# K and V by seven products of blocks for pairs of head groups, in a cross-attention and feed-forward block on one core

## The chip, the cores and the metric

One core of one Trainium2 chip runs the whole program; nothing is sharded. The metric is the device time of one run in microseconds, the median of the runs shown. Five engines work side by side, each through its own list of instructions in order: PE (TensorE, matmuls), DVE (VectorE), ACT (ScalarE), POOL (GpSimd) and SP (SyncE, which here only issues transfers). They wait for each other by semaphores.

## The reference

Four sequences (`B`) of 512 rows of width 512, 16 heads of 32, and a feed-forward width of 2048, all in f32:

```
q = (layer_norm(x, ln1) @ q_w + q_b)          # heads of 32
k = (encoder @ k_w + k_b)
v = (encoder @ v_w + v_b)
attn = softmax(where(mask, q k^T / sqrt(32), min))
hidden = (attn v) @ cproj_w + cproj_b + x
y = gelu(layer_norm(hidden, ln2) @ fc_w + fc_b)
out = hidden + y @ proj_w + proj_b
```

## The kernel before

The 16 heads of a sequence form four groups of four heads, 128 columns of Q, K and V each; `w` counts groups over all four sequences, 0 to 15, so groups 0 to 3 are sequence 0. The context `eT` and the normalized rows `xT` lie transposed in `ext`, the weights of a group in `ptt` (`kqv_w`, two slots each for K, Q and V), K and Q of four groups in `pbt` (`k_q`), V of five groups in `mix` (`v_of`).

For each group K, Q and V are made with four matmuls of 512 columns for K and Q (L475, L487) and sixteen of 128 columns for V (L497). ACT copies K and Q with their bias (L477, L489) and V (L502) out of the bank, and POOL adds V's bias (L330). For each of four blocks of 128 query rows, PE then makes the scores of four heads, one bank each of `sc` (L510); DVE adds the mask and takes the maximum (L518), ACT the exponential and its sum (L521); DVE transposes in blocks of 32 (L529, L536, L539) into one of two buffers, half a group each. POOL copies the blocks that stay on their partitions (L546, the stay step), SP's transfers exchange the others, and PE multiplies with V (L568), which DVE scales (L574).

After a sequence's attention come the output projection (L443), the second normalization with its transposes (L369), and the feed-forward layer. The latter already uses seven products of blocks where plain blocks would take eight: `a_sums` and `b_sums` form sums of blocks of both operands, four each (the weights' on POOL, L330 and L333, the rows' on DVE); `fc` makes seven products of 128 x 256 x 256, five in one bank as a chain whose value is read out after the first, third, fourth and fifth, and two in another; `joins` copies the chain at each of those points on ACT (L646, L651) and adds the other bank on DVE. A product of the chain may only be added once the copy ahead of it has read the bank. A chunk of 256 hidden columns is joined in a `stage` buffer, goes through gelu (L667) there, and leaves for DRAM (L669); three such buffers go round. Four `acc` banks serve everything but the scores. The last layer (`project`) uses such products on two levels.

The order in which every engine's instructions are written is one long table, `ORDER`: a token names a step and each time that it appears the step's generator runs on by one `yield`. Since each engine works in order, the table fixes what stands ahead of what.

Of the kernel before, what the change touches and what calls it, by code (L numbers as in the profile page):

```python
# [12 lines left out]
F32 = mybir.dt.float32  # L13
# [47 lines left out]
s1:0 k:0 s1:0 s1:0 s1:0 r1:0 n1:0 n1:0 n1:0 n1:0 wq:1 wv:1 k:0 v:0 k:1 k:1 qb t1:0:1 t1:0:1 t1:0:0 t1:0:3 t1:0:0  # L61
  t1:0:2 m:0 t1:0:2 t1:0:3 q:0 q:0
u:0:0 x:0:0 x:0:0 x:0:0 x:0:0 q:1 r:0:0
u:0:1 r:0:0 lx:1 lf:0:0 lf:0:0 wq:2 wv:2 v:1 wk:3 wk:2 lx:1 lx:1 lc wv:3 lf:0:2 v:0 x:0:1 x:0:1 x:0:1 x:0:1 r:0:1
  r:0:1 q:1
u:0:2 r:0:1 r:0:1 q:2 x:0:2 x:0:2 x:0:2 x:0:2
u:0:3 r:0:2 x:0:3 x:0:3 v:1 x:0:3 v:3 x:0:3
u:1:0 k:3 v:2 e:0:0 e:0:0 e:0:0 lh:0 lh:0 wq:3 r:0:2 r:0:3 r:0:3 lx:1 wv:5 m:0 d:0:0 v:1 d:0:0 x:1:0 s1:1 r:0:3 r:0:3
  e:0:1 e:0:1 e:0:1 v:3 s1:1 x:1:0 x:1:0 x:1:0 r:1:0 r:1:0
u:1:1 k:2 x:1:1 x:1:1 x:1:1 v:2 x:1:1 k:2 r:1:1 s1:1  # L70
u:1:2 r:1:1 q:2 s1:1 x:1:2 x:1:2 x:1:2 x:1:2 k:3 d:0:1 d:0:1 v:0 fs:0:0 r:1:2 r:1:1 q:3
u:1:3 r1:1 a:0:0 ts:1 r:1:1 x:1:3 ts:1 le:1 wk:4 wq:4 wk:5 lt:1 lt:1 le:1 le:1 le:1 a:0:1 a:0:0 x:1:3 e:1:0 ts:1 k:4
# [12 lines left out]
u:4:0 k:7 d:3:0 d:3:0 a:2:1 r:3:2 r:3:3 r:3:3 m:1 r:3:3 r:3:3 x:4:0 x:4:0 x:4:0 x:4:0
u:4:1 r:4:0 v:7 x:4:1 x:4:1 x:4:1 v:6 e:3:1 e:3:1 wv:9 e:3:1 lf:0:2 x:4:1 v:6
u:4:2 r:4:0 r:4:1 a:3:0 x:4:2 x:4:2 k:7 r:4:1 a:3:0 x:4:2 r:4:1 r:4:1 x:4:2 c:0:1 d:3:1 v:4 d:3:1
u:4:3 r:4:2 c:0:0 a:3:1 x:4:3 x:4:3 q:7 x:4:3 c:0:1 r:4:3 x:4:3 c:0:0
u:5:0 r:4:2 r:4:3 x:5:0 x:5:0 a:3:1 x:5:0 x:5:0 c:0:2
u:5:1 c:0:3 s2:0 r:4:3 wk:8 lh:0 d:4:0 cb:0 c:0:2 s2:0 s2:0 r:4:3 le:2 lx:2 le:2 lf:0:1 wq:6 s1:2 wk:9 lh:0 e:4:0  # L90
  e:4:0 e:4:0 le:2 le:2 c:0:0 v:7 fs:0:0 fs:0:0 cb:0 d:4:0 fs:0:1 x:5:1 c:0:3 fs:0:0 m:1 v:6 c:0:1 d:4:1 e:4:1 q:6
  wv:8 e:4:1 e:4:1 d:4:1 x:5:1 r:5:0 x:5:1 x:5:1 a:4:0
u:5:2 v:9 k:8 s2:0 r:5:0 x:5:2 r2:0 r:5:1 n2:0 r:5:1 n2:0 r:5:1 r:5:1 q:6 x:5:2 x:5:2 k:8 x:5:2 c:0:2 c:0:3 n2:0
u:5:3 a:4:0 n2:0 x:5:3 t2:0:1 t2:0:1 r:5:2 t2:0:0 t2:0:0 x:5:3 r:5:2 x:5:3 k:9 a:4:1 x:5:3 r:5:3 v:9 k:9 y:0
u:6:0 x:6:0 d:5:0 fs:0:1 fs:0:1 d:5:0 t2:0:3 t2:0:2 x:6:0 t2:0:2 x:6:0 x:6:0 a:4:1 v:8 f:0:0 t2:0:3 j:0:0 r:5:3 r:5:3
  y:0
u:6:1 y:0 f:0:0 f:0:1 f:0:0 e:5:0 lx:2 wk:10 lx:2 s1:2 lt:2 lt:2 e:5:0 e:5:0 lf:0:3 r:5:3 e:5:1 lx:2 x:6:1 y:0 v:8
  r:6:0 x:6:1 f:0:1 j:0:0 f:0:0 x:6:1 j:0:0 j:0:1 x:6:1 r:6:0
u:6:2 f:0:1 j:0:1 j:0:0 f:0:0 f:0:1 j:0:0 x:6:2 s1:2 r:6:1 r:6:1 j:0:1 f:0:2 fs:0:1 fs:0:2 d:5:1 fs:0:2 s1:2 r1:2
  x:6:2 j:0:1 f:0:1 j:0:1 x:6:2 j:0:0 x:6:2 r:6:1 ts:2 a:5:0 a:5:0 j:0:1 r:6:1  # L100
u:6:3 g:0:0 g:0:0 ts:2 g:0:1 x:6:3 x:6:3 j:0:2 lf:0:4 e:5:1 wk:11 lt:2 lf:0:4 e:5:1 wv:10 wq:8 e:6:0 fs:0:2 d:5:1 k:10
  ts:2 fs:0:2 fs:0:3 lb:2 e:6:0 lb:2 d:6:0 fs:0:3 d:6:0 f:0:2 f:0:2 r:6:2 x:6:3 x:6:3 r:6:2 r:6:3 j:0:2 k:10 r:6:3
  r:6:3
u:7:0 f:0:2 j:0:2 x:7:0 x:7:0 x:7:0 x:7:0 a:5:1
u:7:1 fs:0:4 e:6:0 v:10 wv:11 lf:0:5 a:5:1 r:6:3 e:6:1 lh:1 lf:0:5 x:7:1 v:10 x:7:1 r:7:0 lt:2 fs:0:4 fs:0:3 na:2
  g:0:0 na:2 na:2 fs:0:4 d:6:1 cb:1 a:6:0 x:7:1 x:7:1 wa:2 r:7:0 r:7:1 j:0:2 a:6:0 r:7:1
u:7:2 f:0:4 j:0:4 x:7:2 f:0:4 f:0:4 x:7:2 j:0:4 f:0:2 f:0:4 j:0:2 x:7:2 wa:2 j:0:4 fs:0:4 f:0:3 x:7:2 j:0:4 f:0:4
  r:7:1 e:6:1
u:7:3 na:2 g:0:1 j:0:4 wa:2 wa:2 g:0:4 r:7:1 j:0:4 q:8 q:8 g:0:4 d:6:1 d:7:0 d:7:0 e:6:1 lf:0:6 lf:0:6 fs:0:6 g:0:4
  f:0:3 lh:1 lh:1 e:7:0 e:7:0 e:7:0 x:7:3 x:7:3 r:7:2 x:7:3 x:7:3 a:6:1  # L110
u:8:0 a:6:1 j:0:2 r:7:3 r:7:2 m:2 x:8:0 r:7:3 j:0:3 x:8:0 v:11 x:8:0 x:8:0 r:7:3 a:7:0 wq:9 wq:10 lx:3
u:8:1 f:0:3 r:7:3 a:7:0 j:0:3 v:11 x:8:1 s1:3 e:7:1 fs:0:3 lf:0:7 e:7:1 e:7:1 r:8:0 x:8:1 d:7:1 cb:1 g:0:1 x:8:1 x:8:1
  r:8:1 c:1:1 c:1:1 f:0:3 g:0:2 q:10
u:8:2 q:9 r:8:0 r:8:1 r:8:1 x:8:2 j:0:3 r:8:1 q:9 x:8:2 q:10 x:8:2 x:8:2
u:8:3 d:7:1 v:8 j:0:3 f:0:3 f:0:5 k:11 x:8:3 x:8:3 r:8:2 r:8:2 j:0:3 e:8:0 wq:11 lf:1:0 e:8:0 le:3 le:3 lh:1 e:8:0
  a:7:1 j:0:3 r:8:3 x:8:3 x:8:3 g:0:3 r:8:3 r:8:3
u:9:0 d:8:0 fs:0:5 fs:0:5 cb:1 d:8:0 fs:0:5 g:0:2 v:10 g:0:2 c:1:1 x:9:0 x:9:0 x:9:0 a:7:1 x:9:0 j:0:5 k:11 c:1:0
  r:8:3 c:1:0
u:9:1 x:9:1 x:9:1 r:9:0 f:0:5 f:0:5 j:0:5 fs:0:5 d:8:1 fs:0:6 fs:0:6 d:8:1 cb:1 s2:1 wk:13 e:8:1 wv:12 lx:3 e:8:1 lx:3
  lf:0:7 lf:1:0 wq:12 e:8:1 wv:13 lf:1:1 f:0:7 f:0:5 c:1:3 j:0:5 r:9:1 x:9:1 x:9:1 j:0:5 f:0:5  # L120
# [119 lines left out]
def xattn_block(ctx: ExitStack, tc: tile.TileContext, x, x_t, encT, mask, q_w, k_w, v_w, c_w, w_fc, p_w, vecs, rows, out):  # L240
# [679 lines left out]
```

## Time and profile before

| what | us |
|---|---|
| median of three runs | 760.3 |
| lowest and highest | 758.3 and 760.86 |
| the profiled execution, its own time | 759.81 |
| its span, first to last instruction | 758.0 |

The granted clock of TensorE is 1.0 throughout the profiled execution. The page gives, per engine, busy time, its share of the span and the number of instructions; PE is the matmuls, PEld the loading of weights, which runs beside them. In the lists of groups a row has line, engine, operation, what is written and read, its shape and count, then busy time and mean duration in ns, then idle time of the engine just ahead of it and what ended that. In the timeline a row begins with start and length; an instruction's recorded length overlaps the next one's, so prices are best read from start to start. The profile counts an f32 matmul of the program as two.

### The profile page before, as it was taken

The page shows a single profiled execution, that of the slowest core. Times are in us where ns is not written, and L with a number is a line of the kernel's source. Part 1 is how long each engine was busy: PE and PEld are TensorE (multiplying, and loading weights), DVE is VectorE, ACT ScalarE, POOL GpSimd, SP SyncE. Part 2 cuts the span into 40 slices and gives each one's busy share as a digit, 9 for nine tenths or more (in the row PEclk, how much of TensorE's full clock was granted, in tenths as well). Part 3 has the DMA queues.
Part 4 walks back from the last instruction along what each step waited for, and adds up shares of the span by engine and source line. Part 5 has one row for each costly group of instructions (what it writes and reads, how often), then busy time and mean ns, then how long its engine had stood idle before and what let it go on. Part 6 is the DMA issues. An engine that isn't in the chain of part 4 may idle for free.

```text
span 758.0 us, 14114 instructions
## 1 busy us (share of the span) xinstructions
PE 751.1 (99%) x4925; PEld 534.0 (70%) x4925; DVE 596.2 (79%) x1209; ACT 403.3 (53%) x951; POOL 371.4 (49%) x401
## 2 busy tenths in 40 slices
PE   9999999999999999999999999999999999999998
PEld 6464555467665456665555677766888999999997
DVE  3798999999768888877778986644689799786982
ACT  2566766456777776778867686861343221211110
POOL 1155864743884656656757657854411022240232
PEclk9999999999999999999999999999999999999999
DMA  7698978877887898784977698789545648788575
GB/s 267 199 240 235 251 212 246 232 193 218 212 236 211 229 251 254 204 246 128 248 221 211 209 271 248 219 277 317 163 140 178 247 134 162 225 169 263 99 180 112
DMA packets 72133, 162.18 MB, mean 214 GB/s; under 512 B 11960, under 2 KB 24656, under 8 KB 70400
## 3 DMA queue, kind: packets, MB, share of 16 engines
q1 hardware_dynamic: 56864, 131.44, 59.7%
q0 software_dynamic: 15056, 29.84, 15.9%
q8 instruction: 39, 0.64, 0.4%
q14 instruction: 30, 0.25, 0.1%
q10 hardware_dynamic: 144, 0.02, 0.0%
HBM read 73.95 MB, written 25.18 MB: 131 GB/s over the span
## 4 chain that ended last, share of the span: by engine, by line
PE 96%; DVE 2%; DMA 1%; issue 0%; POOL 0%; ACT 0%; POOLq 0%; DVEq 0%
PE acc L621 37%; PE sc L621 11%; PE sc L510 9%; PE acc L475 8%; PE acc L487 8%; PE acc L443 7%; PE acc L568 7%; PE acc L497 7%; PE acc L369 1%; DMA pbt<-fc_w_dram 1%; PE acc L850 1%; DVE ext L333 0%; DVE swap L330 0%; DVE yT L330 0%; DVE xn L330 0%
## 5 line engine op out<-in xcount | busy, mean ns | idle before, releaser
L521 ACT ACTIVATE ptt<-ptt,mn 128x512 f32<-128x512 f32 x256 | 182.9, 716 | 78.0 <-DVE mn L518 77.5
L518 DVE CUSTOM_DVE_ANT_0 ptt<-sc,mix 128x512 f32<-128x512 f32 x256 | 164.6, 680 | 30.5 <-PE sc L510 29.1
L546 POOL COPY swap<-swap 32x1088 f32<-32x1088 f32 x128 | 139.8, 1092 | 70.0 <-DVE swap L539 43.9
L529 DVE STREAM_TRANSPOSE swap<-ptt 128x1024 f32<-128x1024 f32 x64 | 78.8, 1232 | 9.5 <-DMA pbt<-fc_w_dram 3.2
L536 DVE STREAM_TRANSPOSE swap<-ptt 128x1024 f32<-128x1024 f32 x64 | 78.3, 1224 | 1.8 <-ACT ptt L521 1.8
L510 PE MATMUL sc<-pbt 32*128 32x512 f32 x512 | 73.8, 640 | 0.8 <-ACT pbt L489 0.8
L669 POOL DMA_DIRECT2D gd<-st x32 | 24.4, 766 | 96.9 <-ACT st L667 87.0
L646 ACT COPY st<-acc 128x256 f32<-128x256 f32 x96 | 34.5, 368 | 69.6 <-PE acc L621 66.3
L497 PEld LDWEIGHTS acc<-ptt,ext 128*128 128x128 f32 x512 | 58.7, 192 | 8.7 <-issue 3.4
L621 PE MATMUL acc<-ys,wsum 128*128 128x256 f32 x256 | 64.1, 382 | 0.0
L568 PE MATMUL acc<-swap,mix 128*32 128x256 f32 x1024 | 61.6, 382 | 0.0
L497 PE MATMUL acc<-ptt,ext 128*128 128x128 f32 x512 | 60.8, 277 | 0.0
L646 ACT COPY xn<-acc 128x128 f32<-128x128 f32 x75 | 18.9, 270 | 77.4 <-PE acc L621 72.5
L621 PE MATMUL acc<-yT,pbt 128*128 128x256 f32 x240 | 58.9, 386 | 1.0 <-DVE mix L574 1.0
L475 PE MATMUL acc<-ext,ptt 128*128 128x512 f32 x128 | 59.1, 605 | 0.0
L487 PE MATMUL acc<-ext,ptt 128*128 128x512 f32 x128 | 58.4, 600 | 0.0
L443 PE MATMUL acc<-mix 128*128 128x512 f32 x128 | 58.0, 600 | 0.0
L621 PEld LDWEIGHTS acc<-yT,pbt 128*128 128x128 f32 x240 | 44.0, 190 | 19.7 <-issue 6.9
L621 PEld LDWEIGHTS acc<-ys,wsum 128*128 128x128 f32 x256 | 47.6, 190 | 12.0 <-POOL wsum L330 1.5
L568 PEld LDWEIGHTS acc<-swap,mix 128*32 128x32 f32 x1024 | 30.6, 109 | 31.4 <-issue 9.0
L330 DVE TENSOR_TENSOR st<-acc,st 128x512 f32<-128x512 f32 (+1 forms) x48 | 26.1, 544 | 32.0 <-ACT st L646 22.4
L521 ACT ACTIVATION_READ_ACCUMULATOR ptt<-ptt,mn 128x1 f32 x256 | 48.3, 189 | 0.0
(143 smaller groups left out, 1396.7 us busy)
## 6 DMA issues: line engine op xcount, KB each, us to landing
swap<-swap SPq DMA_DIRECT2D x384, 136.0 KB, 3.4
gd<-st POOLq DMA_DIRECT2D x32, 512.0 KB, 4.7
swap<-gd SPq DMA_DIRECT2D x12, 1024.0 KB, 5.8
pbt<-fc_w_dram SPq DMA_DIRECT2D x40, 256.0 KB, 4.3
xn<-x_dram SPq DMA_DIRECT2D x32, 256.0 KB, 5.3
ext<-fc_w_dram SPq DMA_DIRECT2D x24, 256.0 KB, 2.9
swap<-xn POOLq DMA_DIRECT2D x18, 256.0 KB, 4.7
ptt<-k_w_dram SPq DMA_DIRECT2D x16, 256.0 KB, 4.0
```

What stands on the lines that cost most here:

```text
L443: nc.tensor.matmul(acc, oT[:, g, ts(t, P)], wc[:, g, :], start=(g == 0), stop=(g == NG - 1))
L475: nc.tensor.matmul(acc, S["wk", w][:, d, :], eT[:, d, :], start=(d == 0), stop=(d == ND - 1))
L487: nc.tensor.matmul(acc, S["wq", w][:, d, :], xT[:, d, :], start=(d == 0), stop=(d == ND - 1))
L497: nc.tensor.matmul(acc[:, ts(t, P)], eT[:, d, ts(t, P)], S["wv", w][:, d, :], start=(d == 0), stop=(d == ND - 1),)
L510: nc.tensor.matmul(sc[h], S["qT", w][r, ts(qt, P)], S["kT", w][r, :], start=True, stop=True)
L518: nc.vector.tensor_tensor_reduce(out=s, in0=sc[h], in1=mb, scale=1.0, scalar=FMAX, op0=ALU.add, op1=ALU.min, accum_out=mn)
L521: nc.scalar.activation(s, s, AF.Exp, bias=mn, scale=-1.0, accum_out=S["sums", w][:, qt, h : h + 1])
L529: nc.vector.transpose(*two_heads[0])
L536: nc.vector.transpose(*two_heads[1])
L546: nc.gpsimd.tensor_copy(pT[ts(i, HD), i], tb[ts(i, HD), i])
L568: nc.tensor.matmul(av[ts(h, HD), : 2 * P].rearrange(shape, **kw), v[:, t, ts(h, HD)], p[t][h], start=(t == 0), stop=(t == NT - 1),)
L621: nc.tensor.matmul(o, x[:, k], y[:, k], start=(k == 0 and not more), stop=(k == n - 1), skip_group_check=more)
```

## The change

Groups 0 and 1 still have K and V made plainly (`prep_k`, `prep_v`). For the seven pairs of groups after them, K of both groups and V of both groups are each made with seven products of blocks (`kv`): the two groups' weights, split in halves of the inner dimension, are one operand, and the context, split in halves of the inner dimension and of the rows, is the other. Q stays plain.

- `e_sums` forms, once a sequence on POOL, four sums of 128 x 512 of the context, three into a new part `es` of `mix` and one over a block of `eT` itself.
- `kv_sums` forms, for K and for V of each pair, four sums of 128 x 256 of the weights on POOL, three into a buffer of the ring `wsums` and one over the loaded weights. `wsums` takes the place of `wsum` and is shared with the feed-forward layer.
- `joins` gets an optional bias. For each pair it makes four copies of 128 x 256 on ACT and two additions on DVE, of 128 x 512 and 128 x 256, for K and the same for V. V's bias is added on POOL as before.
- K and Q of four groups keep their place, in another arrangement; V now has room for four groups, as two pairs, where it had five.
- `stage` has two buffers in place of three.
- Some sums of the last layer lie elsewhere; the fourth sum for its product 2 is made in two halves.
- `ORDER` is written anew.

```diff
 ORDER = """
...
-u:0:2 r:0:1 r:0:1 q:2 x:0:2 x:0:2 x:0:2 x:0:2
...
+u:0:2 ks:1 vb:0 ks:1 r:0:1 v:1 vj:1 r:0:1 pv:1 x:0:2 x:0:2 x:0:2 es:0 m:0 vs:1 es:0 ks:1 es:0 k:1 es:0 vs:1 x:0:2 vs:1
...
-    stage = Ring(const.tile([P, 2 * L], F32, tag=f"st{i}", name=f"st{i}") for i in range(3))
+    stage = Ring(const.tile([P, 2 * L], F32, tag=f"st{i}", name=f"st{i}") for i in range(2))
...
-    v_of = [mix[:, i * D : (i + 1) * D].rearrange("p (t f) -> p t f", t=NT) for i in range(5)]
+    v_of = [mix[:, i * 2 * D : (i + 1) * 2 * D] for i in range(2)]
...
+    es = mix[:, 27 * D // 2 : 33 * D // 2].rearrange("p (s i l) -> p s i l", s=3, i=2)
...
-    wsum = const.tile([P, 2, 3, 2, P], F32, tag="wsum", name="wsum")
+    wsums = Ring(const.tile([P, 3, 2, P], F32, tag=f"ws{i}", name=f"ws{i}") for i in range(2))
...
+    def e_blocks():
+        return [eT[:, 2 * k : 2 * k + 2, j * HL : (j + 1) * HL] for k in range(2) for j in range(2)]
+
+    def e_sums(b):
+        e = e_blocks()
+        return b_sums(nc.gpsimd, *e, es[:, 0], es[:, 1], e[1], es[:, 2])
+
+    def kv_sums(name):
+        def take(p):
+            a = [kqv_w(2 * p + i, "kqv".index(name)) for i in range(2)]
+            s = S["s" + name, p] = wsums.take(name, p)
+            return a_sums(nc.gpsimd, a[0][:, :2], a[0][:, 2:], a[1][:, :2], a[1][:, 2:], s[:, 0], s[:, 1], a[1][:, :2], s[:, 2])
+
+        return take
+
+    def kv(name):
+
+
+        def product(o, x, y, more=False):
+            for t in range(2 if name == "v" else 1):
+                for k in range(2):
+                    i, j = (y[:, k, ts(t, P)], x[:, k]) if name == "v" else (x[:, k], y[:, k])
+                    out_ = o[:, ts(t, P)] if name == "v" else o
+                    nc.tensor.matmul(out_, i, j, start=(k + t == 0 and not more), stop=(k == 1), skip_group_check=more or t > 0)
+
+        def take(p):
+            a, b = [kqv_w(2 * p + i, "kqv".index(name)) for i in range(2)]
+            e11, t3, e21, e22 = e_blocks()
+            t1, t2, t4 = (es[:, i] for i in range(3))
+            chain = S["qa", name, p] = accs.take("qa", name, p)[:, :HL]
+            product(chain, a[:, :2], e11)
+            yield
+            s = S["s" + name, p]
+            q = S["qc", name, p] = halves(accs.take("qc", name, p))
+            product(q[:, 0], a[:, 2:], e21)
+            product(q[:, 1], b[:, :2], t3)
+            yield
+            product(chain, s[:, 1], t2, True)
+            yield
+            product(chain, s[:, 0], t1, True)
+            yield
+            product(chain, s[:, 2], e22, True)
+            product(q[:, 1], b[:, 2:], t4, True)
+            wsums.done(name, p)
+
+        return take
+
+    def k_join(p):
+        kT = k_q(2 * p, 0)
+        for i in range(2):
+            S["kT", 2 * p + i] = kT[:, i * D : (i + 1) * D]
+        b = [bias("k", 2 * p + i) for i in range(2)]
+        return joins(kT.rearrange("p (i n) -> p i n", i=4), ("k", p), True, (b[0], b[0], b[1], b[1]))
...
-    def joins(g, key, own):
+        wsums.done("f", b, c)
+
+    def joins(g, key, own, biases=None):
+
+        def copy(i):
+            if biases is None:
+                nc.scalar.copy(g[:, i], S["qa", *key])
+            else:
+                nc.scalar.activation(g[:, i], S["qa", *key], AF.Identity, bias=biases[i], scale=1.0)
 
         for i in (0, 2, 3):
-            nc.scalar.copy(g[:, i], S["qa", *key])
+            copy(i)
             yield
         q = S["qc", *key]
         add(nc.vector, g[:, 0:4:3], q, g[:, 0:4:3])
         yield
-        nc.scalar.copy(g[:, 1], S["qa", *key])
+        copy(1)
         accs.done("qa", *key)
         yield
         add(nc.vector, g[:, 2], q[:, 1], g[:, 2])
```

How the order moves is seen at three places. First PE, where K and V of groups 2 and 3 are made. Before, K of group 3, V of group 2 and K of group 2 stand around the second and third block of scores of group 1 (`x4` and `x16` are equal rows put together; L475 is K, L497 V, L510 scores):

```order
L475 MATMUL acc_78<-ext,ptt 128x512 x4
L497 MATMUL acc_81<-ptt,ext 128x128 x16
L510 MATMUL sc_74<-pbt 128x512
L510 MATMUL sc_75<-pbt 128x512
L510 MATMUL sc_76<-pbt 128x512
L510 MATMUL sc_77<-pbt 128x512
L475 MATMUL acc_80<-ext,ptt 128x512 x4
L510 MATMUL sc_74<-pbt 128x512
L510 MATMUL sc_75<-pbt 128x512
L510 MATMUL sc_76<-pbt 128x512
L510 MATMUL sc_77<-pbt 128x512
```

After the change, the pair of groups 2 and 3 from the third block of scores of group 0 to the first of group 1 (L524 is a product, L581 scores; `ws` holds sums of weights, `mix` sums of the context):

```order
L524 MATMUL acc_79<-ptt,ext 128x128 x4
L524 MATMUL acc_81<-ext,ptt 128x256 x4
L581 MATMUL sc_74<-pbt 128x512
L581 MATMUL sc_75<-pbt 128x512
L581 MATMUL sc_76<-pbt 128x512
L581 MATMUL sc_77<-pbt 128x512
L524 MATMUL acc_80<-ptt,ext 128x128 x8
L524 MATMUL acc_78<-mix,ws_109 128x256 x2
L524 MATMUL acc_79<-ws_110,mix 128x128 x4
L524 MATMUL acc_78<-mix,ws_109 128x256 x2
L524 MATMUL acc_79<-ws_110,mix 128x128 x4
L581 MATMUL sc_74<-pbt 128x512
```

The products of a pair stand in four pieces with scores between them, V's (128 columns) and K's (256 columns) in turn, and both take two banks at once.

Second DVE, in group 2, from the second block's first maximum on (L518 or L589 with a read of the maximum behind each). Before:

```order
L518 ISA ptt,mn_1_0_606<-sc_74,mix 128x512
L518 ISA mn_1_0_606 128x1
L518 ISA ptt,mn_1_1_633<-sc_75,mix 128x512
L518 ISA mn_1_1_633 128x1
L529 STREAM_TRANSPOSE swap<-ptt 128x2x4x4x32
L518 ISA ptt,mn_1_2_670<-sc_76,mix 128x512
L518 ISA mn_1_2_670 128x1
L529 STREAM_TRANSPOSE swap<-ptt 128x2x4x4x32
L518 ISA ptt,mn_1_3_674<-sc_77,mix 128x512
L518 ISA mn_1_3_674 128x1
L536 STREAM_TRANSPOSE swap<-ptt 128x2x4x4x32
```

After:

```order
L589 ISA ptt,mn_1_0_649<-sc_74,mix 128x512
L589 ISA mn_1_0_649 128x1
L332 TENSOR_TENSOR pbt<-acc_79,pbt 128x2x256
L589 ISA ptt,mn_1_1_684<-sc_75,mix 128x512
L589 ISA mn_1_1_684 128x1
L610 STREAM_TRANSPOSE swap<-mix 128x2x4x32
L600 STREAM_TRANSPOSE swap<-ptt 128x2x4x4x32
L589 ISA ptt,mn_1_2_690<-sc_76,mix 128x512
L589 ISA mn_1_2_690 128x1
L589 ISA ptt,mn_1_3_693<-sc_77,mix 128x512
L589 ISA mn_1_3_693 128x1
L607 STREAM_TRANSPOSE swap<-ptt 128x2x4x4x32
```

Between the maxima there is now a wide addition of a join, here K of a pair into `pbt`.

Third POOL, at the start, up to the first copies of the stay step (L546, then L617). Before:

```order
L349 TENSOR_SCALAR ve_0_157<-mv_0_140 128x4
L357 TENSOR_TENSOR rs_0_159<-ve_0_157,nhalf 128x4
L454 DMA m_73<-mask_dram 128x512
L546 COPY swap<-swap 32x1088 x2
L330 TENSOR_TENSOR mix<-mix,row 128x512
L546 COPY swap<-swap 32x1088 x6
L330 TENSOR_TENSOR mix<-mix,row 128x512
```

After:

```order
L335 TENSOR_TENSOR mix<-ext 128x512
L456 DMA m_73<-mask_dram 128x512
L332 TENSOR_TENSOR ws_110<-ptt 128x256
L335 TENSOR_TENSOR mix<-ext,mix 128x512
L335 TENSOR_TENSOR ws_109<-ws_109,ptt 128x256
L335 TENSOR_TENSOR ext<-ext 128x2x256
L335 TENSOR_TENSOR mix<-ext,mix 128x512
L335 TENSOR_TENSOR ptt<-ptt 128x256
L335 TENSOR_TENSOR ws_110<-ws_110,ptt 128x256
L335 TENSOR_TENSOR ws_110<-ptt,ws_110 128x256
L335 TENSOR_TENSOR ws_109<-ptt,ws_109 128x256
L617 COPY swap<-swap 32x1088 x8
```

Twelve sums of the context and of the weights, and V's first bias, now stand ahead of the first copies; the first two sums and the bias stand just ahead of the rows shown.

426 lines of the change are left out of this document (230 added, 196 removed).

## The prediction

> **What bounds the kernel now.** I read the page first, then the chain of waits, then the busy time by stretches, then the waits of VectorE (DVE) in the stretch that matters, and last the timeline, for prices.
>
> ```profile
> span 758.0 us, 14114 instructions
> PE 751.1 (99%) x4925; PEld 534.0 (70%) x4925; DVE 596.2 (79%) x1209; ACT 403.3 (53%) x951; POOL 371.4 (49%) x401
> PE 96%; DVE 2%; DMA 1%; issue 0%; POOL 0%; ACT 0%; POOLq 0%; DVEq 0%
> ```
>
> By the whole span TensorE (PE) sets the time: it is busy for 99% and makes up 96% of the chain that ended last. But a share of the span is a mean over stages. Between the first scores of group 0 and the first scores of group 6 it looks different:
>
> ```profile
> 22.91 1.14 PE L510 MATMUL sc<-pbt 32*128 32x512 f32 x8 [0.78 <-ACT pbt L489]
> 24.07 0.69 DVE L518 CUSTOM_DVE_ANT_0 ptt<-sc,mix 128x512 f32<-128x512 f32 x1 [4.53 <-PE sc L510]
> 165.49 0.68 DVE L518 CUSTOM_DVE_ANT_0 ptt<-sc,mix 128x512 f32<-128x512 f32 x1
> 166.83 1.14 PE L510 MATMUL sc<-pbt 32*128 32x512 f32 x8
> 22.91:166.83 143.92, 143.92 (x929) 74.36 (x930) 133.72 (x298) 91.35 (x230) 84.89 (x83) 1.00 0.83 231
> 24.07:166.10 142.03, 142.03 (x913) 73.73 (x917) 132.99 (x296) 90.62 (x228) 84.54 (x83) 1.00 0.84 231
> DVE ptt L518 <- PE sc L510: 10.9, 14, 4.5
> DVE rsum L533 <- ACT ptt L521: 1.0, 1, 1.0
> DVE mix L574 <- PE acc L568: 0.8, 2, 0.5
> ```
>
> The columns of the two stretches are length, then busy time of PE, weight load, DVE, ACT and POOL. From the first scores of group 0 (22.91) to those of group 6 (166.83) PE works without a pause, 143.9 us; DVE works for 133.0 of the 142 us from its first maximum to the last one of group 5. What DVE waits for is nearly all PE (10.9 and 0.8 us, 4.5 of it ahead of the first maximum); ACT has 1.0 us. So DVE here is 9 us away from being the bound, while over the page it seems 21% away. The link back is the score bank: tile row q of the scores goes into the same four banks that row q-1 was read from, so PE can't write the scores of group 6 before DVE has taken the last maximum of group 5.
>
> **The change part by part.** Prices of PE, each from start to next start:
>
> ```profile
> 350.99 7.03 PE L487 MATMUL acc<-ext,ptt 128*128 128x512 f32 x16
> 357.95 1.93 PE L568 MATMUL acc<-swap,mix 128*32 128x256 f32 x32
> 110.16 3.70 PE L487 MATMUL acc<-ext,ptt 128*128 128x512 f32 x8
> 113.79 1.14 PE L510 MATMUL sc<-pbt 32*128 32x512 f32 x8
> 119.56 3.84 PE L497 MATMUL acc<-ptt,ext 128*128 128x128 f32 x32
> 123.33 1.14 PE L510 MATMUL sc<-pbt 32*128 32x512 f32 x8
> 546.51 1.89 PE L621 MATMUL sc<-yT,ext 128*128 128x256 f32 x8
> 548.24 1.89 PE L621 MATMUL acc<-ys,wsum 128*128 128x256 f32 x8
> ```
>
> The profile counts each f32 matmul of the program twice. Sixteen of 512 columns take 6.96 us (350.99 to 357.95), eight take 3.63: this fits 0.429 us each plus 0.1 us at a change between the full array and the 32-wide tiles of scores and attention. Then 32 of 128 columns take 3.77, less two changes 0.1116 each. Eight of 256 columns take 1.73, 0.216 each: two of them are no dearer than one of 512.
>
> *K*: two groups take 16 x 0.429 = 6.87; seven products of two halves take 28 x 0.216 = 6.05. Seven pairs save 7 x 0.82 = 5.7. *V*: 64 x 0.1116 = 7.14 against 56 x 0.1116 = 6.25, seven pairs save 6.2. In the two order lists PE changes between full array and tiles 138 times before and 140 times now, +0.2. PE's work falls by 11.7 us.
>
> What comes for it on DVE are two joins for each of 14 results. Prices:
>
> ```profile
> 553.16 0.69 DVE L330 TENSOR_TENSOR st<-sc,st 128x512 f32<-128x512 f32 x1 [0.62 <-ACT st L646]
> 553.77 0.68 DVE L333 TENSOR_TENSOR pbt<-pbt 128x512 f32<-128x512 f32 x1
> 557.30 0.42 DVE L330 TENSOR_TENSOR st<-sc,st 128x256 f32<-128x256 f32 x1
> 557.64 0.42 DVE L333 TENSOR_TENSOR wsum<-ext,wsum 128x256 f32<-128x256 f32 x1
> ```
>
> 0.61 and 0.34 us, start to start: 0.95 a result, 13 us in all. After group 7 PE has far more to do per group (feed-forward work comes in) and hides this; up to group 6 nothing does. I counted both lists over the stretch. *PE*, first scores of group 0 to first scores of group 6: K goes from 32 instructions of 512 columns (27.5 us) to 50 of 256 (21.6), V from 128 to 100 of 128 columns (28.6 to 22.3), eight transposes of the second normalization move out (1.8), one small transpose moves in (0.2); queries, attention and output projection are alike. 143.9 - 5.9 - 6.3 - 1.8 + 0.2 = 130.1. *DVE*, first maximum to last maximum of group 5: 96 maxima, 46 large and 11 small transposes and nine attention products in both; 7 wide joins (4.2) and 6 narrow ones (2.0) come in, three statistics steps too (2.3, at 0.77), four normalizations (1.8, at 0.46) and one scaled copy out of a bank (0.7) go out. 133.0 + 6.0 = 139.0.
>
> DVE starts 1.2 after the first scores, so it lets go of the last bank 140.2 us after them at best; PE wants that bank at 130.1, plus 0.8 since it is the fourth of the row: PE stands idle for 9.3 us. I add 0.5, half of the 1.0 that DVE waits for ACT: 9.8. This idle time is spread over groups 2 to 5 and can't be won back, since PE's later work is all still to do. Bounds: with the prices alone (maxima 0.61 each, transposes 1.16) DVE's list sums to 138.3 and PE's to 131.6, both a little off the trace, which gives 7.0; if DVE keeps the share of waiting that it has now, 133.0 of 142, it needs 148.5 and the idle time is 19. I take 9.8, near the low end, because the waits in the rows above are PE's own doing and vanish once PE is early.
>
> ACT: 56 copies of 256 columns in place of 28 of 512, with the exponentials among them. From the rows below, 56 x 0.37 against 14 x 0.68 + 14 x 0.57 is +3.2 us on an engine that is busy for 91 of 144 us in the stretch: nothing, as long as a copy isn't queued behind a late exponential; PE's next product of the chain waits for it, and behind that all else on PE.
>
> ```profile
> L646 ACT COPY st<-acc 128x256 f32<-128x256 f32 x96 | 34.5, 368 | 69.6 <-PE acc L621 66.3 <-DMA gd<-st 3.3
> L477 ACT ACTIVATE pbt<-acc,vec 128x512 f32<-128x512 f32 x16 | 10.9, 679 | 12.9 <-PE acc L475 12.9
> L502 ACT COPY mix<-acc 128x512 f32<-128x512 f32 x16 | 9.1, 571 | 2.2 <-PE acc L497 2.1
> L330 POOL TENSOR_TENSOR mix<-mix,row 128x512 f32<-128x512 f32 x16 | 20.4, 1273 | 11.1 <-ACT mix L502 5.9 <-issue 4.6
> L330 POOL TENSOR_TENSOR wsum<-pbt 128x256 f32<-128x256 f32 x20 | 14.7, 740 | 24.3 <-PE acc L621 19.3 <-DMA pbt<-fc_w_dram 4.3 <-POOL swap L546 0.3
> 559.75 0.65 ACT L646 COPY st<-acc 128x256 f32<-128x256 f32 x2 [1.44 <-DMA gd<-st]
> 554.28 1.03 PE L621 MATMUL sc<-ys,ext 128*128 128x256 f32 x4
> ```
>
> POOL: 16 sums of the context at 1.27 us (20.4) and 56 sums of weights at 0.74 (41.4), 62 us. In the stretch there are 12 and 28 of them, 36 us on top of 84.9: 121 of some 141. Costed at nothing, hidden by POOL's waiting; uncovered it is the rival below. Two stage buffers: a chunk's last product began at 554.28 and its buffer was free at 559.75, 4.6 us after the product's end at 555.15. In the list of the change the least PE work between a chunk's last product and the step that needs its buffer is 7.0 us (9.5 before): nothing.
>
> Sum: 758.0 - 11.7 + 9.8 = 756.1 of span. The profiled run took 759.8, so 1.8 lie around the span: 757.9. The median of the runs shown, 760.3, is 0.5 above the profiled one: **758.4 us**.
>
> **The rivals.** *The whole gain*: DVE's deficit is hidden, and 760.3 - 11.7 = 748.6. For it: 99% on PE, 79% on DVE over the span. Against it: the stretch, where DVE's list is longer than PE's.
>
> *DVE bounds the whole, slower*: then nothing of PE's gain arrives and the 13 us of joins are added: 760.3 + 13.3 = 773.6. For it: 133 of 142 us in the stretch. Against it: after the stretch DVE idles for 92 us of 373, PE for one.
>
> ```profile
> 167.00:540.00 373.00, 371.82 (x2235) 239.43 (x2236) 280.68 (x601) 260.86 (x565) 237.98 (x268) 1.00 0.80 230
> ```
>
> [...]
>
> *POOL comes late, slower*: POOL works in order, and in its list the first twelve sums of context and weights stand ahead of the first copies of group 0 (L546, the stay step), which before had next to nothing ahead of them. DVE can't turn group w+1 into a buffer until POOL has copied group w out of it; DVE is the bound, so each microsecond so lost is lost for good. If a third of the 36 us falls there, +12: 770.4. It decides the sign from 4.2 us on, an eighth of them. For it: 86% load on an engine that waits for others. Against it: POOL waits for DVE now, not DVE for POOL, in this stretch.
>
> *Two buffers are too few, slower*: eight of the late chunks have under 11 us between last product and reuse. If the hand-over took 10 us and not 4.6, the shortest (9.2, 7.0, 9.6, 8.8, 7.9) would lack 0.8 + 3.0 + 0.4 + 1.2 + 2.1 = 7.5: 765.9. Against it: 3.3 us of waiting for these transfers in the whole of before.
>
> That the change doesn't do what it says can't be: the list has the 98 + 196 instructions.
>
> **How the numbers follow.** Forecast 0.63, whole gain 0.10, DVE throughout 0.03, POOL 0.16, buffers 0.08. I call 0.3% of 760.3 (2.3 us) what can't be told from no change, so faster is below 758.0 and slower above 762.6. The forecast lies on that edge: of its 0.63 I give 0.28 to faster (idle 7 to 9.4), 0.30 to same, 0.05 to slower (idle over 14). The whole gain adds 0.10 to faster; DVE throughout 0.03 to slower; POOL 0.02 to same and 0.14 to slower; the buffers 0.03 and 0.05. Faster 0.38, same 0.35, slower 0.27. The forecast's own range is 755.6 (idle 7.0) to 767.6 (idle 19); with part of the rivals, 752 to 768.
>
> **What would show it.** Right: in the profile of the change PE waits in groups 2 to 5 for DVE's maxima (L589), some 10 us in all, with DVE busy for over 95% there, and no PE wait of note after group 7; PE's work 11.7 us shorter. Wrong: no such waits (the whole gain); DVE's transposes waiting for POOL copies (L617); PE waiting for ACT copies that wait for a transfer out of a stage buffer. It would also be wrong if the chained copies on ACT, queued behind exponentials, hold PE more than the banks do.

## The result, and the profile after

The changed kernel takes **764.18 us** (median of 15 runs, 760.19 to 770.07), the kernel before 759.94 us on the same chip (15 runs, 757.87 to 761.09). The ratio is 1.0059, 95% interval 1.0042 to 1.0076: **0.6% slower**. The forecast was 758.4 us, 1.9 below the 760.3 known then, with the sign left nearly open.

Three rows of the changed kernel's page, the same ones with which the prediction began: the span, the busy time of the engines, and the chain of work that ended last by engine.

```profile
span 763.5 us, 14364 instructions
PE 750.3 (98%) x4953; PEld 548.2 (72%) x4953; DVE 614.5 (80%) x1238; ACT 411.4 (54%) x981; POOL 431.5 (57%) x473
PE 87%; DMA 4%; DVE 3%; ACT 3%; SPq 1%; issue 1%; POOL 0%; DVEq 0%; POOLq 0%; ACTq 0%
```

PE's share of the chain that ended last fell from 96% to 87%. PE's busy time fell by 0.8 us only, although 11.7 us of products are gone. The costliest groups of instructions of the changed kernel show where it went (count, then busy time in us, mean ns of one, idle time before it):

```profile
L581 PE MATMUL sc<-pbt 32*128 32x512 f32 x512 | 82.0, 647 | 0.0
```

The same 512 score records took 73.8 us before (at line 510 there). They have next to no idle time ahead of them in either kernel (0.8 us before, 0.0 now); they are stretched, and what stretches them counts as busy. So 0.8 us is no measure of PE's work, and the span has to be cut at marks that both kernels have: the first scores of groups 0, 6 and 7. The view is busy time by stretches of the changed kernel; the columns are start and end, length, then PE, weight load, DVE, ACT and POOL, the granted clock, the DMA share and GB/s:

```profile
23.10:167.20 144.10, 139.17 (x903) 77.69 (x902) 137.66 (x308) 90.37 (x240) 107.42 (x113) 1.00 0.85 229
167.20:201.70 34.50, 32.03 (x192) 20.28 (x188) 32.52 (x66) 22.92 (x52) 27.37 (x28) 0.95 0.75 217
201.70:763.50 561.80, 557.38 (x3770) 435.41 (x3769) 437.22 (x849) 292.84 (x685) 291.38 (x322) 1.00 0.73 207
```

and two stretches of the kernel before that the prediction did not show, between the same marks:

```profile
166.80:197.40 30.60, 30.56 (x193) 21.76 (x189) 28.83 (x63) 22.80 (x55) 12.89 (x17) 1.00 0.79 211
197.40:758.00 560.60, 555.86 (x3722) 424.00 (x3721) 426.62 (x835) 284.40 (x661) 270.83 (x292) 1.00 0.75 209
```

From group 0 to group 6: 144.1 us, as long as before (143.9), although PE's list there is some 13 us shorter. From group 6 to 7: 34.5 for 30.6, although the list there is some 2 us shorter too (both are counted further down). From there to the end: 561.8 for 560.6. The saving is gone before group 7; behind it PE is busy without a break to speak of, as forecast, but it has more of its work still ahead of it.

The timeline of the changed kernel shows how a block of scores is stretched. First PE (start, duration, engine, line, operation):

```profile
56.42 1.14 PE L581 MATMUL sc<-pbt 32*128 32x512 f32 x8
60.42 3.18 PE L581 MATMUL sc<-pbt 32*128 32x512 f32 x8
63.53 0.70 PE L524 MATMUL acc<-ext,ptt 128*128 128x256 f32 x2
```

and DVE in the same time:

```profile
58.35 0.69 DVE L589 CUSTOM_DVE_ANT_0 ptt<-sc,mix 128x512 f32<-128x512 f32 x1
59.09 1.19 DVE L607 STREAM_TRANSPOSE swap<-ptt 128x1024 f32<-128x1024 f32 x1
60.20 0.65 DVE L589 CUSTOM_DVE_ANT_0 ptt<-sc,mix 128x512 f32<-128x512 f32 x1
60.78 0.44 DVE L610 STREAM_TRANSPOSE swap<-mix 128x256 f32<-128x256 f32 x1
61.15 0.65 DVE L589 CUSTOM_DVE_ANT_0 ptt<-sc,mix 128x512 f32<-128x512 f32 x1
61.73 0.69 DVE L589 CUSTOM_DVE_ANT_0 ptt<-sc,mix 128x512 f32<-128x512 f32 x1
```

At 56.42 four heads are scored side by side in 1.14 us, because all four banks were free. DVE then takes the four maxima at 58.35, 60.20, 61.15 and 61.73, with transposes between them. PE comes back at 60.42 and gets the banks one by one; the block takes 3.18 us, 2.04 more, and the K product behind it waits. PE is "busy" all the time.

Is this DVE's own pace, or does DVE wait too? The stretch of the changed kernel from the first maximum to the last one of group 5, same columns:

```profile
24.30:167.53 143.23, 138.30 (x896) 77.58 (x898) 137.98 (x308) 90.53 (x240) 106.56 (x112) 1.00 0.85 229
```

DVE (the third engine) is busy for 137.98 of 143.23 us and idle for 5.2.

### The profile page after: what moved, and what is told of

The parts are those of the page before. It is cut to its first block, busy times and chain, and to the rows that moved or that the text cites. A ratio compares the mean times of both kernels' runs of the same rounds, so it can differ in the third digit from the quotient of the medians.

```text
span 763.5 us, 14364 instructions
## 1 busy us (share of the span) xinstructions
PE 750.3 (98%) x4953; PEld 548.2 (72%) x4953; DVE 614.5 (80%) x1238; ACT 411.4 (54%) x981; POOL 431.5 (57%) x473
## 4 chain that ended last, share of the span: by engine, by line
PE 87%; DMA 4%; DVE 3%; ACT 3%; SPq 1%; issue 1%; POOL 0%; DVEq 0%; POOLq 0%; ACTq 0%
PE acc L694 36%; PE sc L694 12%; PE acc L524 9%; PE sc L581 8%; PE acc L445 7%; PE acc L639 6%; PE acc L573 5%; DMA ext<-encT_dram 2%; SPq L329 1%; ACT ptt L592 1%; PE acc L371 1%; DVE ptt L589 1%; PE acc L481 1%; PE acc L492 1%; DMA gd<-st 1%
## 5 line engine op out<-in xcount | busy, mean ns | idle before, releaser
L589 DVE CUSTOM_DVE_ANT_0 ptt<-sc,mix 128x512 f32<-128x512 f32 x256 | 165.4, 678 | 21.3 <-PE sc L581 18.6
L617 POOL COPY swap<-swap 32x1088 f32<-32x1088 f32 x128 | 140.2, 1095 | 36.1 <-DVE swap L610 29.6
L720 ACT COPY st<-acc 128x256 f32<-128x256 f32 x128 | 46.1, 367 | 96.3 <-PE acc L694 85.7
L720 ACT COPY xn<-acc 128x128 f32<-128x128 f32 x100 | 24.1, 267 | 133.0 <-PE acc L694 129.3
L581 PE MATMUL sc<-pbt 32*128 32x512 f32 x512 | 82.0, 647 | 0.0
L694 PE MATMUL acc<-ys,ws 128*128 128x256 f32 x256 | 63.4, 383 | 0.5 <-ACT st L720 0.5
L573 PE MATMUL acc<-ext,ptt 128*128 128x512 f32 x128 | 58.8, 600 | 1.4 <-DVE mn L589 0.8
L694 PEld LDWEIGHTS acc<-ys,ws 128*128 128x128 f32 x256 | 47.4, 190 | 13.1 <-ACT st L720 4.7
L906 POOL DMA_DIRECT2D swap<-xn x18 | 22.4, 1434 | 52.8 <-DVE xn L332 18.7
L906 POOL DMA_DIRECT2D yT<-xn x15 | 18.3, 1547 | 48.5 <-DVE yT L332 17.9
L573 PEld LDWEIGHTS acc<-ext,ptt 128*128 128x128 f32 x128 | 23.3, 190 | 30.9 <-issue 23.3
L445 PEld LDWEIGHTS acc<-mix 128*128 128x128 f32 x128 | 23.2, 190 | 31.0 <-issue 28.6
```

Of the source, the lines that this page charges most:

```text
L445: nc.tensor.matmul(acc, oT[:, g, ts(t, P)], wc[:, g, :], start=(g == 0), stop=(g == NG - 1))
L573: nc.tensor.matmul(acc, S["wq", w][:, d, :], xT[:, d, :], start=(d == 0), stop=(d == ND - 1))
L581: nc.tensor.matmul(sc[h], S["qT", w][r, ts(qt, P)], S["kT", w][r, :], start=True, stop=True)
L589: nc.vector.tensor_tensor_reduce(out=s, in0=sc[h], in1=mb, scale=1.0, scalar=FMAX, op0=ALU.add, op1=ALU.min, accum_out=mn)
L617: nc.gpsimd.tensor_copy(pT[ts(i, HD), i], tb[ts(i, HD), i])
L694: nc.tensor.matmul(o, x[:, k], w, start=(k == 0 and not more), stop=(k == n - 1), skip_group_check=more)
```

## The experiments

Twelve kernels ran. The first theory was that of the prediction: up to group 6 DVE's list, made longer by the joins, is what PE waits for. Ratios are to the kernel before.

### Plain products in the changed order

The written order, the layout of K and V and the two stage buffers stay; K and V come from plain products that take the places of the seven, once for all pairs and once for pairs 1 to 3 alone:

```
+PLAIN_KV = (1, 2, 3, 4, 5, 6, 7)        # second kernel: (1, 2, 3)
 def take(p):
+    return plain(name, p) if p in PLAIN_KV else seven(p)
...
+    part(o, w[0], 0); yield              # first half of group 2p
+    part(o, w[0], 1); yield
+    part(o, w[1], 0); yield              # group 2p + 1
+    part(o, w[1], 1); yield
```

> The changed written order and the two stage buffers are kept, but K and V of all groups are made by plain products (no sums on POOL, no joins on DVE). Theory (DVE's list is longer than PE's in groups 1 to 6 because of the joins): PE's work is 11.7 us longer again (758.0 us), DVE's list in the stretch is some 6 us shorter than in the changed kernel and so under PE's, and the 17 us of waiting nearly go: 758 to 762 us, ratio to before 0.997 to 1.003. Rival (the new order or the two stage buffers make the waits): the waits stay on top of the longer work, 768 to 776 us.

> The changed order and buffers; pairs 1 to 3 (groups 2 to 7) plain, pairs 4 to 7 (groups 8 to 15) by seven products. Theory: 4/7 of the 11.7 us of PE work stay saved (PE work 751.3 us) and PE waits as in the kernel before, about 1 us: 753 to 756 us, ratio 0.991 to 0.996, faster than both. Rival (joins cost DVE time that PE waits for in the later groups too): 758 to 764 us.

Measured: 776.61 us, ratio **1.0234** (1.021 to 1.0259), and 768.84 us, ratio **1.0121** (1.0102 to 1.0141). Both fell on the side of the rival, and even above its ranges (768 to 776 and 758 to 764). With not one product of seven in it, the changed order is 17.8 us slower than the kernel before (0.0234 x 760), while the arithmetic is that of before. The products put back for pairs 4 to 7 bring 0.0113, 8.6 us; those of pairs 1 to 3 bring 0.0062, 4.7 us. Together 13.3 us with some 2 us of doubt each way, where the prediction had 11.7 for PE's work alone: **in this order the products, with their joins, save about what was forecast, early and late**. The all-plain kernel by stretches, between the same marks and with the same columns:

```profile
23.60:173.20 149.60, 147.14 (x887) 73.47 (x886) 133.58 (x299) 89.82 (x229) 78.37 (x78) 0.99 0.78 220
173.20:205.90 32.70, 29.57 (x184) 18.03 (x180) 30.25 (x61) 20.97 (x47) 22.57 (x23) 0.95 0.80 220
205.90:774.80 568.90, 563.56 (x3766) 432.00 (x3765) 428.88 (x835) 291.71 (x672) 267.95 (x291) 1.00 0.72 204
```

and two rows of its waits from 24 to 200 us (who waits, for whom: us in total, times, longest):

```profile
DVE ptt L644 <- PE sc L636: 15.6, 9, 5.4
PEld sc L636 <- DVE mn L644: 7.6, 15, 1.0
```

DVE's busy time up to group 6 is 133.6 us, as in the kernel before; the stretch takes 149.6. DVE waits for PE's scores (15.6 us, of which 5.4 lie ahead of the first maximum), and PE waits for DVE's maxima (its scores take 81.6 us again, as in the changed kernel). Each has enough time in sum, and each waits for the other in turn. The first theory falls as the whole cause: these waits need no joins.

One reserve: the order was written for five steps of seven products, and two plain products in the places of four of them are not what it was balanced for. So 17.8 us is the price of this order with plain products made pair by pair in it, not of the order by itself.

### The joins and the sums taken out

```
+NO_ADDS = [(n, p) for n in "kv" for p in (1, 2, 3)]
+if key not in NO_ADDS:                   # both joins
     add(nc.vector, g[:, 0:4:3], q, g[:, 0:4:3])
```

```
 def take(p):                             # kv_sums; e_sums likewise for sequences 0 and 1
+    if p < 4: return None
...
-t1, t2, t4 = (es[:, i] for i in range(3))
+t1, t2, t4 = (es[:, i] for i in range(3)) if p > 3 else (e11, e21, e22)
```

> The changed kernel without DVE's join additions for K and V of pairs 1 to 3 (so K and V there lack a part of the products); POOL's sums, ACT's copies and PE's products stay. 12 additions, 5.7 us of DVE, go. Theory: PE's waits up to group 6 shrink by 5.7 us or a little more: 756 to 759 us, ratio 0.995 to 0.999. Rival (POOL's sums and copies are late): 763 to 765 us, unchanged.

> The changed kernel without POOL's sums for pairs 1 to 3 (the products of these pairs take unsummed blocks in their place, as many and of the same size); DVE's joins stay. Theory: no more than 2 us less, from DVE instructions that POOL slows down beside it: 761 to 765 us, ratio 1.002 to 1.007. Rival (POOL comes late): 752 to 757 us.

Measured: without the early joins 762.02 us, ratio 1.0027 (1.0009 to 1.0046); without the early sums 764.58 us, 1.0075 (1.0047 to 1.0103). The first lies between the theory (756 to 759 us) and the rival (763 to 765), the second in the theory's range. Against the 1.0059 of the changed kernel, the 5.7 us of joins are worth 2.4 us, give or take 2, and POOL's sums nothing. The kernel without the early joins up to group 6:

```profile
22.30:163.60 141.30, 138.33 (x903) 77.60 (x902) 132.09 (x296) 90.08 (x239) 109.61 (x115) 1.00 0.84 234
```

what DVE waits for in it up to the first scores of group 7 (195.9 us):

```profile
DVE ptt L591 <- PE sc L583: 7.5, 6, 4.5
```

and the same row of the changed kernel, up to the same mark (201.7 us):

```profile
DVE ptt L589 <- PE sc L581: 5.5, 6, 4.5
```

DVE's busy time fell by 5.6 us (137.66 to 132.09) and the stretch by 2.8, so half of what is taken from DVE turns into idle time of DVE, most of it waiting for scores (2.0 us more). In both rows 4.5 us lie ahead of the first maximum: behind it DVE waits for scores for 1.0 us in the changed kernel, for 3.0 without the joins. POOL as the late engine is out: the kernel without its sums is no faster, and in the changed kernel POOL waits for DVE. One wait of PE there does name a sum of POOL, 1.3 us; without the sums the stretch up to group 7 still takes 177.1 us, for 178.6 in the changed kernel.

### The same DVE work added at three places

Twelve statistics over 512 columns (0.69 us each in the traces, 8.3 us) stand between maxima and exponentials; a tile that nothing reads takes their result.

```
+if w in EXTRA and qt < 3 and h == 0:     # EXTRA: groups 2-5, or 9-12
+    nc.vector.bn_stats(extra, row[:, 0, :])
 nc.scalar.activation(s, s, AF.Exp, bias=mn, scale=-1.0, ...)
```

> The changed kernel with 12 more DVE statistics of 512 columns (0.67 us each, 8.1 us; their result is used by nothing) among the score maxima of groups 2 to 5. Theory now (in groups 1 to 6 PE and DVE wait for each other in turn, block by block, as the written order sets it): nearly all of it comes out as time, 769 to 772 us. Rival (DVE does not bound these groups): 764 to 766 us.

> The same 12 statistics among the score maxima of groups 9 to 12 of the changed kernel. Theory: DVE waits for PE there, so nothing: 763 to 765.5 us. Rival (DVE bounds the whole kernel): 770 to 772 us.

> The kernel before with the same 12 statistics among the score maxima of groups 2 to 5. If only the sums of the two lists count (PE 143.9 us, DVE 133.0 us up to group 6, room for 8.1 us): 760 to 761 us, no change. If PE and DVE are coupled block by block: a part comes out, 762 to 766 us. If DVE bounds there as well: 768 us.

Measured, as ratio and as us beyond the kernel that it was added to: early in the changed kernel 1.0115 (1.0102 to 1.0128), +4.3; late in it 1.0066 (1.0049 to 1.0083), +0.5, not to be told from 1.0059; early in the kernel before 1.0041 (1.0025 to 1.0056), +3.1. Late work on DVE is free within some 2 us, so **DVE does not bound the whole**. Early work costs half of itself in the changed kernel and a good third in the kernel before, where by the two lists there was room for all of it. The sums of the lists alone don't decide; how PE's and DVE's steps meet counts in both kernels. The first expectation (nearly all of it) was too high, and so was the like one for the joins.

Up to group 7 the kernel with the late statistics does step by step what the changed kernel does, so its trace shows how far two traces of the same steps differ. Its two early stretches, same marks and columns:

```profile
22.51:164.53 142.02, 138.91 (x903) 77.78 (x902) 137.15 (x307) 90.44 (x240) 109.46 (x115) 1.00 0.85 232
164.53:197.76 33.23, 31.51 (x193) 19.89 (x189) 31.43 (x67) 22.79 (x52) 25.15 (x26) 1.00 0.83 225
```

142.0 and 33.2 us, for 144.1 and 34.5: a difference of 2 us between stretches of two traces, such as the 2.8 above, shows little by itself, and the medians have to bear it out.

### Another order of the same instructions

The 732 steps ahead of group 8 were written in another order, for the changed kernel and for the two kernels with plain products. It was drawn up from the durations of PE, DVE, ACT and POOL, with one time from issue to landing put in for every transfer, a guess of the author's that no trace shows. One of the 32 blocks that begin with a `u` step, before and after:

```
-u:1:2 ts:1 ts:1 e:0:1 e:0:1 x:1:2 r:1:1 r:1:1 x:1:2 r:1:1 e:0:1 ks:2 ts:1 ks:2 ks:2 k:2 a:0:0 q:2 x:1:2 x:1:2 a:0:0 d:1:0
+u:1:2 k:2 e:0:1 d:0:1 r:1:1 wv:4 es:1 ks:2 d:0:1 x:1:2 r:1:1 kj:2 ts:1 x:1:2 x:1:2 ts:1 es:1 a:0:0 x:1:2 e:0:1 e:0:1 r:1:1
```

> The changed kernel, every product, sum and addition as it is; only the written order of the 732 steps between the first scores of group 0 and those of group 8 is another (steps moved by a few places, what they compute unchanged). Theory: the waits of groups 1 to 6 (17 us) come from where the order puts DVE's and PE's work, not from the products; where DVE is never without work up to group 6 they fall by the 4 us it waits there, and by some 3 us more in group 6: 756 to 760 us, ratio 0.995 to 1.001. Rival (the joins' DVE time itself makes the waits, in whatever order): 762 to 765 us.

> As products_late_only (pairs 1 to 3 plain, 4 to 7 by seven products), with the steps ahead of group 8 in another order. Theory: its waits (16 us) shrink as above, and it lands where the mended changed kernel does or a little lower, since the 5 us of PE work that it has more lie where PE waits for DVE anyway: 756 to 761 us. Rival (PE's work counts in full there): 5 us above the mended changed kernel.

> As order_plain_all (no products), with the steps ahead of group 8 in another order. Theory: 6 to 9 us of its 16 us of waits go, 767 to 771 us; it does not come back to 760 us, because more PE work than in the kernel before is left over for the time after group 7 (571 us from there in order_plain_all, 561 us before). Rival (order alone, all of it to be mended in these steps): 758 to 762 us.

Measured: 780.41 us, ratio 1.0269 (1.0247 to 1.0291); 798.57 us, 1.0494 (1.0462 to 1.0526); 792.99 us, 1.0435 (1.0414 to 1.0456). All three missed, by 16 to 30 us against the kernels that they started from. A row of the waits of SP's queue in the first 200 us of the first of them (us in total, times, longest):

```profile
SPq L330 <- DVE swap L611: 34.1, 6, 9.0
```

and the same row of the changed kernel:

```profile
SPq L329 <- DVE swap L610: 11.0, 6, 2.9
```

SP works through its list in order: in the changed kernel's trace none of its 650 issues begins before the one ahead of it has ended. Exchanges had been moved ahead of the transposes that they wait for, and loads of weights stood behind them; the exchanges take 3.5 us from issue to landing here (the median of 384), longer than was guessed. That this is what cost the time was not tested by itself. So this set says nothing for or against a better order. It does show that one order of the *same* instructions and another differ by 16 us, more than all the products are worth.

### The order of the kernel before in the changed layout

Up to the first scores of group 10 the steps stand as in the kernel before, with plain K and V; from there the changed order goes on, with pairs 6 and 7 by seven products. V of single groups has five places there, and the room that holds sums of weights only from group 9 on serves as a third stage buffer until then. A second kernel moves 93 steps where the two orders meet.

```
+spare = mix[:, 27 * D // 2 : 31 * D // 2]
+stage.free.append(spare)
+v_slots = [mix[:, i * D : (i + 1) * D] for i in range(4)] + [mix[:, 31 * D // 2 : 33 * D // 2]]
...
+v = S["v", w] = v_slots[w % 5].rearrange("p (t f) -> p t f", t=NT)
```

> The steps up to the first scores of group 10 stand in the written order of the kernel before, with K and V of pairs 1 to 5 plain; behind that the changed order goes on, with pairs 6 and 7 by seven products. Layout of K, V and the sums as in the changed kernel; the place of the sums of encoder blocks serves as fifth V buffer and third stage buffer until then. PE's work is 758.0 - 2/7 x 11.7 = 754.7 us. Theory (the changed written order of the groups before the feed-forward makes the waits): they are gone, with up to 6 us of new ones where the two orders meet: 757 to 763 us. Rival (layout, or the order behind group 10, makes them): 768 us or more.

> As old_order_to_10, with 93 steps of PE, DVE and ACT between groups 9 and 12 moved by a few places, so that DVE's statistics of two normalizations do not stand ahead of the score maxima where the two orders meet; no load, exchange or step of POOL is moved. Theory: 754.7 us of PE work and 1 to 3 us of waits and 1.8 us around the span: 756 to 760 us, at or under the kernel before. Rival as above: 768 us or more.

Measured: 773.11 us, ratio 1.0171 (1.0147 to 1.0196), and 763.85 us, 1.0054 (1.0031 to 1.0077). In time the first fell on the side of the rival (768 us or more), the second between theory (756 to 760) and rival, but the stretches of the second kernel (same marks, same columns) tell the two halves apart:

```profile
22.60:166.60 144.00, 143.97 (x933) 74.41 (x933) 133.79 (x298) 91.39 (x230) 84.84 (x83) 1.00 0.84 231
166.60:197.10 30.50, 30.47 (x193) 21.70 (x189) 28.64 (x63) 22.72 (x55) 12.87 (x17) 1.00 0.76 209
197.10:766.30 569.20, 559.58 (x3730) 429.42 (x3729) 432.02 (x844) 285.53 (x667) 288.88 (x312) 1.00 0.74 206
```

Up to group 7 PE is busy for 174.44 of 174.5 us, as in the kernel before (143.89 and 30.56 of 174.5). The new places of K and of the weight sums are in this kernel: they make no wait, and **with the old order the early waits are gone**. Two parts of the new layout are not in it that early, though: V has five places of single groups there and not four by pairs, and there are three stage buffers and not two. Nor are K and V made pair by pair there. So the early waits come from the order or from what it was written for; which of these was not taken apart. Behind group 7 the kernel takes 8.6 us more than before (569.2 for 560.6), although pairs 6 and 7 save PE 3.3 us by the prices of the prediction. (The traced run took 768.07 us, 4.2 above the median, so up to half of the 8.6 may belong to that run.) Where the two orders meet, statistics and normalizations of two sequences fall into group 10 together: its scores wait again (at 292.35 and 298.31 their blocks take 2.2 and 1.8 us longer than the usual one). So no version here is faster than the kernel before.

## Why the prediction was wrong

*PE's saving, 11.7 us*: borne out. In one and the same order the seven products brought 13.3 us, give or take 2, and that with their joins on DVE in the path.

*The joins on DVE, 13 us, hidden from group 7 on*: right in price and place. They take 0.69 and 0.41 us of busy time, work added in groups 9 to 12 costs nothing that can be told, and behind group 7 PE is busy for 557.4 of 561.8 us (555.9 of 560.6 before).

*The idle time of PE, 9.8 us*: this is **the step that failed**. The span is 763.5 us where the kernel before less PE's saving has 746.3: PE lost 17.2 us, 7.4 more than forecast. The stretches put it in two places.

Up to group 6, 13.1 us. PE's list there is 131.0 us and not 130.1, since the eight transposes that move out were priced at 1.8; in the kernel before they take 1.09:

```profile
167.90 1.09 PE L369 MATMUL acc<-ident,xn 128*128 128x128 f32 x8
```

(0.93 from start to start; these are the eight right behind the mark, those ahead of it take as long). The stretch takes 144.1. DVE's list was right: 137.98 us of busy time plus 0.6 for the last maximum, against 139.0. What was wrong is DVE's waiting: 0.5 us was put for it, on the ground that DVE's waits "are PE's own doing and vanish once PE is early", and 5.2 us came. The waits for scores did nearly vanish (6.4 us behind the first maximum before, 0.9 now); others came in their place, 1.0 us for ACT's copies of the joins, the rest in pieces of under a microsecond. In the trace of the same steps with the late statistics the stretch takes 142.0, so 11.0 are lost there: this part alone missed by 1 to 3 us.

From group 6 to 7, another 5.8 us, where the prediction put nothing: it had PE idle in groups 2 to 5 only. By its own prices the list there is some 1.9 us shorter than before (in records of the profile: 12 of 256 columns of the feed-forward layer and 32 of V fewer; one multiplication with V, 8 of products and 8 transposes more), and the stretch is 3.9 us longer. The four normalizations and eight transposes that the prediction took out of the stretch up to group 6 stand here, and PE waits for them; the last section has the rows. Behind group 7 some 2 us come back.

*That the joins make these waits* is right in small part only. Without the early joins the stretches are 141.3 and 32.3 us, so by the same lists some 10 and 4 us are still lost, and the time falls by 2.4. With plain products in it the new order loses 17.8 us and the products with their joins bring 13.3 back: +4.5, the 0.6%. With the old order, and K and V made plainly for one group after the other, nothing is lost up to group 7. *That the rewritten order as such costs nothing* was never written as a term, and was assumed. A likely reading, not shown block by block: with one set of four score banks neither engine can be more than one block ahead, so a block where DVE has more than PE costs PE time, and the next one, where PE has more, doesn't give it back. The added statistics fit it: in the kernel before the lists leave room for 8.3 us of them, and 3.1 come out as time.

*"In groups 2 to 5 PE waits for DVE's maxima, DVE over 95% busy, no wait behind group 7"*: so it is seen (137.66 of 144.1 us is 95.5%), but plain products show stretched scores too, with DVE busy for 89%. The sign that was to show the forecast right was there, and the time still went up: what the sign stands for explains 2.4 us.

*The rivals*, with POOL's row in the waits of the changed kernel's first 200 us:

```profile
POOL swap L617 <- DVE swap L610: 14.9, 4, 6.1
```

The whole gain, no. DVE bounds the whole, no: the late statistics cost nothing that can be told. POOL late, no: without its sums the time is the same, and POOL's row reads "waits for DVE". Two buffers too few: ACT does wait longer for transfers out of a stage buffer, 10.5 us in the changed kernel,

```profile
ACT st L720 <- DMA gd<-st: 10.5, 7, 4.0
```

where the kernel before had 3.3; but PE's idle time behind group 7 that is put down to these copies is 0.5 us. A third buffer for the late chunks was not tried by itself.

Open: which of the moved steps make the early waits, whether V's four places by pairs or the making by pairs has a part in them, and whether the seven products of the early pairs would keep their 4.7 us in an order that has none. An order that holds both was not found.

## What to carry to other kernels

Where two engines hand each other one set of buffers, the difference of their totals over a long stretch is only the least that the engine with the shorter list loses (up to group 6 the prediction's lists gave 9.3 us, and 11.0 to 13.1 were lost): put a price on the waits of the other one too. Work that is counted as moving out of a stretch has to be followed to where it lands; here it landed right behind it, and PE waited there (5.8 us lost between groups 6 and 7). When a change comes with a rewritten order, run the new order with the old arithmetic first; here that one kernel put +17.8 and -13.3 us apart, which in the sum looked like a small loss. Trace the same steps twice before a difference of 2 us between stretches is explained. And before PE's busy time is believed, look at the mean of its groups: blocks that wait for their banks one by one count as busy (82.0 us of scores for 73.8).

## What the runs showed of the hardware

*A normalization beside POOL*. The timeline of DVE in the changed kernel, behind group 6's first row of scores:

```profile
168.15 0.91 DVE L364 TENSOR_SCALAR xn<-xn,mv,rs 128x512 f32<-128x512 f32 x1
169.59 3.49 DVE L364 TENSOR_SCALAR xn<-xn,mv,rs 128x512 f32<-128x512 f32 x3
```

and a row of the same view of the kernel before:

```profile
158.44 0.54 DVE L362 TENSOR_SCALAR xn<-xn,mv,rs 128x512 f32<-128x512 f32 x1
```

0.54 us before, while POOL waits; 0.91 and 1.16 (a third of 3.49) now, while POOL is busy beside it (1.20 of 1.20 us in the first of the four stretches below, which begins inside the last of these). The whole trace of the changed kernel has 20 such normalizations: the eight with sums or copies of POOL beside them take 0.85 to 1.31 us, the other twelve 0.53 to 0.55. What makes them longer was not tested.

*The clock in a run of transposes and waits*. PE in the changed kernel behind these normalizations:

```profile
171.16 0.38 PE L371 MATMUL acc<-ident,xn 128*128 128x128 f32 x2
171.90 0.33 PE L371 MATMUL acc<-ident,xn 128*128 128x128 f32 x1 [0.35 <-DVE xn L364]
173.13 0.77 PE L371 MATMUL acc<-ident,xn 128*128 128x128 f32 x5 [0.91 <-DVE xn L364]
174.33 1.85 PE L371 MATMUL acc<-ident,xn 128*128 128x128 f32 x8 [0.43 <-ACT yT L381]
176.11 2.01 PE L581 MATMUL sc<-pbt 32*128 32x512 f32 x8
```

and four stretches of it (the granted clock is the eighth column, ahead of the DMA share):

```profile
171.90:173.10 1.20, 0.32 (x1) 0.13 (x1) 1.20 (x2) 0.00 (x0) 1.20 (x2) 1.00 0.00 0
173.10:174.30 1.20, 0.77 (x5) 0.53 (x5) 1.20 (x2) 0.80 (x2) 1.14 (x3) 1.00 0.02 3
174.30:175.20 0.90, 0.87 (x5) 0.81 (x6) 0.90 (x3) 0.90 (x2) 0.82 (x2) 0.61 0.00 0
175.20:176.10 0.90, 0.90 (x5) 0.58 (x3) 0.90 (x6) 0.90 (x3) 0.35 (x1) 0.50 0.00 0
```

From 171.16 to 174.33 PE has nothing but transposes (1.5 us) and three waits (1.7 us, the longest 0.91). Then the granted clock falls to 0.5: eight transposes take 1.85 us, and the scores 2.01 for 1.14 with all banks free. The kernel before does eight of these transposes in 1.09 us, right behind a block of scores (the row at 167.90 above), and its clock from group 6 to 7 stays at 1.00. What brings the clock down was not tested. In the kernel with the late statistics, the same steps run at a granted clock of 1.00 from group 6 to 7, so the fall doesn't come in every run.

The 5.8 us lost between groups 6 and 7 add up from these rows and two others:

```profile
167.24 2.17 PE L581 MATMUL sc<-pbt 32*128 32x512 f32 x8
198.11 3.67 PE L573 MATMUL acc<-ext,ptt 128*128 128x512 f32 x8 [0.78 <-DVE mn L589]
```

The block at 167.24 gets its banks one by one, 1.0 us. The sixteen transposes with their waits take from 171.16 to 176.11, 4.95 us for 1.86 at the pace of the kernel before, 3.1. The block at 176.11 loses 0.87, and ahead of 198.11 there are 0.78 more.

*The spread*. The 15 runs of the changed kernel lie within 9.9 us, those of the kernel before within 3.2. Nothing here tells why.
